# Expert up-weights kept on chip and copied per tile by an engine, instead of loaded per tile by DMA

## The chip, the cores and the metric

One core of a Trainium2 chip runs the kernel. The metric is the device time of one execution in microseconds (us). Five engines work side by side, each through its own list of instructions in order, and meet at semaphores: TensorE (PE, matrix products; PEld is its loading of weights), VectorE (DVE), ScalarE (ACT), GpSimd (POOL) and SyncE (SP, which here issues most DMAs). DMA engines move data between the chip's memory (DRAM) and the on-chip memory (SBUF). PE writes to PSUM, from which DVE and ACT read.

## The reference: what is computed

Eight sequences of 512 tokens with 128 features, all in float32, go through three layers, each with a residual: a routed feed-forward layer, a gated linear recurrence, and the same feed-forward layer again.

```
x = x + 0.5 * ffn(layernorm(x))
x = x + attn(layernorm(x))
x = x + 0.5 * ffn(layernorm(x))

def ffn(x):                                  # 8 experts, one per token
    xn  = rms_norm(x, scale)
    ids = argmin(dist2(xn, centroids))
    out = zeros_like(x)
    for e in range(8):
        a, g = split(xn @ up_w[e])           # up_w[e]: 128 x 512
        y = (a * silu(g)) @ down_w[e]        # down_w[e]: 256 x 128
        out = where(ids == e, y, out)
    return out + x
```

`attn` forms r, k, v by one product, takes exp(k), runs two decaying sums along the sequence, divides one by the other, multiplies by sigmoid(r) and projects.

## The kernel before

**Tokens are sorted by expert through DRAM.** `prepare` (L580) computes norms, scores and a row for each token of 260 values: its normalised features, half of its layer-norm output and residual, and its number. `route` (L647) finds each token's expert and its place in a table in DRAM; `scatter` (L714) writes 128 rows at a time there with an indirect DMA issued by POOL. `take` (L729) then divides the table into tiles of 128 rows that belong to one expert each and writes, for each tile, one integer to `place`: the tile's number plus 512 times its expert.

**Experts.** `experts` (L817) loads `place` into registers (L826), on SP for the loads and on PE for the down weights. `pair` (L847) handles two tiles at once:

- SP loads the tiles' rows to `xg` (L866, 130 KB a tile, 7 buffers of a pair) and their experts' up weights to `wup` (L873, 256 KB a tile, 3 buffers of a pair), both from addresses in registers;
- PE transposes the features (L879), ACT evicts them to `xgT` (L907);
- PE multiplies by the up weights (L884, eight products a tile, to the PSUM tile `h`);
- ACT applies silu (L916), DVE multiplies (L921), giving `sg`;
- PE multiplies by the down weights (L892, four products a tile), which all lie in SBUF (`wsb`) and are picked by PE's registers; the one PSUM area for it has room for one pair;
- DVE adds the half-residual (L928) and POOL scatters each tile's result to its tokens' places in DRAM (`send`, L934).

There are three tables: one for blocks (sequences) 0 to 3 and one for 4 to 7 in the first layer, with 23 tiles each, and one for all of the last layer with 39 tiles, of which 8, 8 and 4 are taken early, as soon as their rows are complete. That makes 85 tiles in 44 pairs. `finish` (L946) loads the blocks back, and `attention` (L953) runs the recurrence, mostly on DVE (L1008 to L1038), ACT and PE.

**The order of each engine's list** is decided at build time by `Plan` (L41 to L154). Each step is added with one or more ways, a way being an engine and an assumed cost, with the buffers it reads and writes, an optional due number per engine (`order`) and a lag. `schedule` places steps one after another where they could start first; a second way is taken only if the first way's engine would be free too late (L101). It tries 48 settings and keeps the shortest plan. Steps due FIRST (such as ACT's and DVE's steps of a pair, `soon`, L859) come ahead of others that could start as early. So the list of an engine after an edit can differ far from the edit.

Of the kernel before, what the change touches and what calls it, by code (L numbers as in the profile page):

```python
# [10 lines left out]
F32 = mybir.dt.float32  # L11
# [29 lines left out]
class Plan:  # L41
# [17 lines left out]
    def add(self, ways, reads=(), writes=(), order=None, part=False, lag=0.0, table=None):  # L59
        op = Op(ways, reads, writes, order or {}, lag, table)  # L60
        for b in reads:
            op.needs.update(b.writers)
            b.readers.append(op)
        for b in writes:
            op.needs.update(b.readers)
            if not (part and not b.readers):
                op.needs.update(b.writers)
            if b.readers or not part:
                b.readers, b.writers = [], []
            b.writers.append(op)  # L70
        op.needs.discard(op)
        self.ops.append(op)
# [85 lines left out]
def kernel(  # L158
# [36 lines left out]
    nc = tc.nc  # L195
    B, L, D = x_in.shape
    E, _, H2 = up_w.shape
    H = H2 // 2
    P = 128
# [22 lines left out]
    const = ctx.enter_context(tc.tile_pool(name="const", bufs=1))  # L222
# [8 lines left out]
    xb = [xpool.tile([P, NT, D], F32, tag=f"x{b}", name=f"x_{b}") for b in range(B)]  # L231

    wsb = const.tile([P, E * W], F32, tag="wsb", name="wsb")
    wrkv_sb = const.tile([P, 3 * P], F32, tag="wrkv_sb", name="wrkv_sb")
    wo_sb = const.tile([P, D], F32, tag="wo_sb", name="wo_sb")

# [17 lines left out]
        out=tri_f, in_=tri_f, pattern=[[-1, P]], compare_op=ALU.is_ge, fill=0.0,  # L254
# [50 lines left out]
    def buf(pool, shape, dtype, tag, n, count):  # L305

        slots[tag] = count
        return Buf(lambda: pool.tile(shape, dtype, tag=tag, name=f"{tag}_{n}", bufs=count), tag)
# [18 lines left out]
    add = plan.add  # L327
    FIRST, LATE = -10**6, 10**6
    EXP, SILU = "natural_log_exp_and_others", "silu_and_others"
    x_ = [Buf(lambda b=b: xb[b]) for b in range(B)]  # L330
    wd_, wr_, wo_, routing_, attending_ = (Buf(lambda w=w: w) for w in (wsb, wrkv_sb, wo_sb, None, None))
    for b in range(B):
        add([("SP", 1.15, lambda b=b: nc.sync.dma_start(
            out=xb[b], in_=x_in[b].rearrange("(t p) d -> p t d", p=P)))], [], [x_[b]], lag=2.5)
    for e in range(E):
        add([("SP", 0.6, lambda e=e: nc.sync.dma_start(
            out=wsb[:, e * W : (e + 1) * W].rearrange("p (c d) -> p c d", d=D),
            in_=down_w[e].rearrange("(c p) d -> p c d", p=P)))], [], [wd_], part=True, lag=2.5)
# [4 lines left out]
        out=bo_f[:, 0, :], in_=b_o.unsqueeze(0).to_broadcast([3, D])))], [], [bo_], lag=2.5)  # L343
# [69 lines left out]
    for j, v in enumerate((nu_log, gamma_log)):  # L413
        add([("ACT", 0.3, lambda j=j, v=v: nc.scalar.dma_start(
            out=arows[j : j + 1, :], in_=v.unsqueeze(0)))], [], [arows_], part=True, lag=2.2)
    add([("ACT", 0.3, lambda: nc.scalar.dma_start(
        out=arows[2:5, :], in_=b_rkv.rearrange("(j p) -> j p", p=P)))],
# [311 lines left out]
    def take(table, m: int):  # L729
# [62 lines left out]
        if last:  # L792
# [13 lines left out]
            add([("SP", 1.3 + 0.52 * E, zeros)], [fills], [fill_], lag=2.5)  # L806
            parts.append(fill_)
        experts(table, m, place, parts)

    def expert(place):  # L810
        return (place >> (PACK.bit_length() - 1)).with_bounds(min_val=0, max_val=E - 1)

    wdown = [wsb[:, c * D :] for c in range(NHC)]
    up_rows = up_w.rearrange("e p h -> p e h")
    npairs = [0]

    def experts(table, m: int, place, parts):  # L817

        downs, downs_ = [], Buf(None)
        spots = {}  # L820
        slots["regs"] = 2

        keep = []

        def load(engine, j0, j1):
            return nc.values_load_multi_w_load_instructions(  # L826
                place()[0:1, j0:j1], engines=(engine,), min_val=0, max_val=(E - 1) * PACK + table.tiles - 1,
                skip_runtime_bounds_check_because="no tile lies beyond the table",
            )[1]

        add([("PE", 0.1 * m, lambda: downs.extend(load(mybir.EngineType.PE, 0, m)))],
            [place], [downs_], {"PE": LATE + npairs[0] * 10 + 5})
        for j0 in range(0, m, LIST):
            j1 = min(j0 + LIST, m)
            at_ = Buf(None, "regs")

            def registers(j0=j0, j1=j1):
                spots.update(zip(range(j0, j1), load(mybir.EngineType.SP, j0, j1)))

            add([("SP", 1.3, registers)], [place], [at_], {"SP": LATE + npairs[0]})  # L840
            for j in range(j0, j1, 2):
                k = npairs[0]
                npairs[0] += 1
                pair(k, table, parts, keep, spots, at_, downs, downs_,
                     list(range(j, min(j + 2, j1))))

    def pair(k, table, parts, keep, spots, at_, downs, downs_, tiles):  # L847
        n = len(tiles)
        early = table.left > 0
        xg = buf(work, [P, 2, ROW], F32, "xg", k, 7)  # L850
        wup = buf(work, [P, 2, H2], F32, "wup", k, WUP)
# [7 lines left out]
        soon = {"ACT": FIRST + k, "DVE": FIRST + k}  # L859
# [12 lines left out]
        def weights(i, j):  # L872
            nc.sync.dma_start(  # L873
                out=wup()[:, i, :],
                in_=up_rows[:, ds(expert(spots[j]), 1), :])

        def features_first():
            for i in range(n):
                nc.tensor.transpose(ps_x()[:, ts(i, P)], xg()[:, i, :D], ident)  # L879
# [17 lines left out]
        for i, j in enumerate(tiles):  # L897
            add([("SP", 0.52, lambda i=i, j=j: rows(i, j))], [at_] + parts, [xg], {"SP": LATE + k},
                part=True, lag=2.3)
        for i, j in enumerate(tiles):  # L900
            add([("SP", 0.52, lambda i=i, j=j: weights(i, j))], [at_], [wup], {"SP": LATE + k},
                part=True, lag=3.8)
        add([("PE", 0.17 * n, features_first)], [xg], [ps_x],
            {"PE": LATE + 10 * k - 13}, lag=0.2)
        add(
# [156 lines left out]
    for i, (f, batches, taken) in enumerate(TABLES):  # L1062
        Table.order = i * LATE // 8
        table = Table(f"t{i}", f, [b for batch in batches for b in batch])
# [44 lines left out]
```

## Time and profile before

| | |
|---|---|
| timed runs, median of 3 | 306.41 us (305.02 to 306.7) |
| the profiled execution | 342.0 us, its recorded span 340.2 us |
| mean granted TensorE clock in it | 0.898 |
| busy in the span | PE 236.0, PEld 197.3, DVE 180.1, ACT 158.8, POOL 178.2 us |
| DMA traffic | 55.83 MB, 164 GB/s on the mean |
| of it, on SP's queue | 42.71 MB |
| up weights | 85 loads of 256 KB |

The profile is of one execution, and that one took longer than the timed runs, so times within it are compared with its own span. It gives, for each engine, what share of the span it was busy, also in 40 slices of 8.5 us as digits (tenths); groups of instructions with count, total and mean time, and the engine's idle time before them; the DMA issues; the waits and who ended them; and a timeline. In a group's name, `h<-xgT,wup` means: writes h, reads xgT and wup. A timeline line gives start, duration (both in us), engine, line, operation and operands, and in brackets how long the engine had been idle and what released it; SPq is SP's queue issuing DMAs. Consecutive alike instructions are merged (x16).

### The profile page before, as it was taken

The numbers are of one execution on the slowest core, as the hardware profiler recorded it, in microseconds if no ns is written. First come the engines' busy times: TensorE is split into PE (matmuls) and PEld (weight loads), VectorE is DVE, ScalarE is ACT, GpSimd is POOL, SyncE is SP. The second block draws the span as 40 slices with busy tenths as digits, with TensorE's granted clock in tenths as the row PEclk, the third lists the DMA queues.
The fourth block names the chain that finished last, engine by engine and source line by source line (L and its number), as shares of the span: only waits on it lengthen the run. The fifth ranks groups of instructions, "written<-read, shape, count | busy, mean of one in ns | idle before, by whom it ended". The sixth has DMA issues, their size and how long they took to land. (4 is left out here: it accounts for less than half of the span.)

```text
span 340.2 us, 5776 instructions
## 1 busy us (share of the span) xinstructions
PE 236.0 (69%) x1510; PEld 197.3 (58%) x1510; DVE 180.1 (53%) x604; ACT 158.8 (47%) x329; POOL 178.2 (52%) x258
## 2 busy tenths in 40 slices
PE   3566167197776995999773867799843495988870
PEld 2565157087666984877451633369742384987770
DVE  4786464121133227559898875989976431232230
ACT  4876652312122231897857385665866131222220
POOL 5377557235544544746271768403677544255563
PEclk9999999679999899999995876989975589899997
DMA  7824586496666799820003217250056578777710
GB/s 212 237 79 160 174 263 204 133 270 191 220 201 204 221 277 323 267 69 18 8 21 104 79 47 263 80 156 15 22 141 228 148 246 286 251 232 219 231 53 8
DMA packets 45139, 55.83 MB, mean 164 GB/s; under 512 B 6255, under 2 KB 31115, under 8 KB 45106
## 3 DMA queue, kind: packets, MB, share of 16 engines
q1 hardware_dynamic: 39286, 42.71, 42.7%
q0 software_dynamic: 5792, 12.73, 10.2%
q8 instruction: 13, 0.21, 0.3%
q14 instruction: 20, 0.16, 0.2%
q10 hardware_dynamic: 28, 0.01, 0.0%
HBM read 39.11 MB, written 17.68 MB: 167 GB/s over the span
## 5 line engine op out<-in xcount | busy, mean ns | idle before, releaser
L884 PE MATMUL h<-xgT,wup 128*128 128x128 f32 x680 | 90.4, 289 | 0.6 <-issue 0.5
L884 PEld LDWEIGHTS h<-xgT,wup 128*128 128x128 f32 x680 | 86.7, 206 | 1.7 <-issue 1.7
L716 POOL DMA_INDIRECT t<-xrow,posi_t x64 | 65.7, 1026 | 35.3 <-issue 17.3
L934 POOL DMA_INDIRECT yt<-ys,xg x46 | 50.8, 1105 | 56.3 <-DVE ys L928 28.1
L921 DVE TENSOR_TENSOR sg<-h,sg 128x512 f32<-128x512 f32 (+1 forms) x44 | 29.1, 670 | 84.7 <-ACT sg L916 65.9
L934 POOL DMA_INDIRECT out_dram<-ys,xg x39 | 39.4, 1009 | 51.5 <-DVE ys L928 36.9
L892 PE MATMUL ps_b<-wsb,sg 128*128 x340 | 49.6, 291 | 21.8 <-DVE ys L928 12.3
L916 ACT ACTIVATE sg<-h 128x512 f32<-128x512 f32 (+1 forms) x44 | 25.2, 582 | 75.5 <-PE h L884 22.9
L892 PEld LDWEIGHTS ps_b<-wsb,sg 128*128 128x128 f32 x340 | 43.8, 201 | 26.9 <-DVE ys L928 14.2
L907 ACT ACTIVATE xgT<-ps_a,cols 128x256 f32<-128x256 f32 (+1 forms) x44 | 20.4, 464 | 47.4 <-PE ps_a L879 24.7
L879 PE MATMUL ps_a<-ident,xg 128*128 128x128 f32 x85 | 20.9, 313 | 20.0 <-ACT xgT L907 10.4
L928 DVE SCALAR_TENSOR_TENSOR ys<-ps_b,xg 128x256 f32<-128x256 f32 (+1 forms) x44 | 18.0, 410 | 24.6 <-PE ps_a L879 10.5
L450 ACT ACTIVATE xrow<-x,nra,rs 128x128 f32<-128x128 f32 x64 | 26.3, 482 | 9.7 <-DVE nra L604 8.3
L622 PE MATMUL ps_b<-cw,xT 128*128 128x8 f32 x128 | 23.0, 312 | 8.3 <-ACT xT L467 4.4
L622 PEld LDWEIGHTS ps_b<-cw,xT 128*128 128x128 f32 x128 | 22.8, 270 | 9.8 <-ACT xT L467 4.9
L879 PEld LDWEIGHTS ps_a<-ident,xg 128*128 128x128 f32 x85 | 11.9, 156 | 25.9 <-ACT xgT L907 13.0
L450 ACT ACTIVATE xrow<-x,nra,one 128x128 f32<-128x128 f32 x64 | 26.1, 480 | 0.0
L689 PE MATMUL ps_b<-onehot_t,tri 128*128 128x32 f16 (+1 forms) x11 | 2.2, 197 | 24.6 <-DVE onehot_t L673 20.8
L152 ACT ACT_TABLE_LOAD x14 | 18.0, 1283 | 0.2
L525 PE MATMUL side_x<-ident,x 128*128 128x128 f32 x64 | 13.6, 354 | 4.9 <-ACT yr L505 2.4
L692 PEld LDWEIGHTS <-ones_h 128*128 128x128 f16 x11 | 1.2, 107 | 26.7 <-issue 26.6
L478 DVE BATCH_NORM_STATS2 bn_f<-x 128x6 f32<-128x128 f32 x64 | 13.6, 281 | 5.0 <-DMA x<-in_L_attn_inputs_dram 3.8
(156 smaller groups left out, 322.8 us busy)
## 6 DMA issues: line engine op xcount, KB each, us to landing
wup<-in_L_ffn_up_w_dram SPq DMA_DIRECT2D x85, 256.0 KB
xg<-t SPq DMA_DIRECT2D x85, 130.0 KB
t<-fill SPq DMA_DIRECT2D x27, 130.0 KB
x<-in_L_attn_inputs_dram SPq DMA_DIRECT2D x8, 256.0 KB
x<-yt SPq DMA_DIRECT2D x8, 256.0 KB
wsb<-in_L_ffn_down_w_dram SPq DMA_DIRECT2D x8, 128.0 KB
t<-xrow,posi_t POOLq DMA_INDIRECT x64
yt<-ys,xg POOLq DMA_INDIRECT x46
```

The source lines that it names most:

```text
L152: self.load_table(load)
L450: nc.scalar.activation(out()[:, t, :], src()[:, t, :], AF.Identity, bias=bias()[:, t : t + 1], scale=scale()[:, t : t + 1],)
L622: nc.tensor.matmul(ps_d()[:, ts(i * NT + t, E)], xT()[:, ts(t, P)], cw, start=True, stop=True)
L716: ordered(table, nc.gpsimd.indirect_dma_start(out=table.at()[:, :], out_offset=bass.IndirectOffsetOnAxis(ap=posi()[:, q : q + 1], axis=0), ...
L879: nc.tensor.transpose(ps_x()[:, ts(i, P)], xg()[:, i, :D], ident)
L884: nc.tensor.matmul(hp()[:, i, ts(c, P)], wup()[:, i, ts(c, P)], xgT()[:, ts(i, P)], start=True, stop=True,)
L892: nc.tensor.matmul(ps_y()[:, ts(i, D)], sg()[:, i, ts(c, P)], wdown[c][:, ds(expert(downs[j]) * W, D)], start=(c == 0), stop=(c == NHC - 1),)
L907: ("ACT", 0.2 + 0.13 * n, lambda: nc.scalar.activation(xgT()[:, : n * P], ps_x()[:, : n * P], AF.Copy, scale=scale_c)),
L916: [("ACT", 0.16 + 0.22 * n, lambda: nc.scalar.activation(sg()[:, :n, :], hp()[:, :n, H:], AF.Silu))],
L921: [("DVE", 0.1 + 0.28 * n, lambda: nc.vector.tensor_mul(sg()[:, :n, :], hp()[:, :n, :H], sg()[:, :n, :]))],
L928: add([("DVE", 0.1 + 0.18 * n, lambda: nc.vector.scalar_tensor_tensor(y()[:, :n, :], half(), 0.5, xg()[:, :n, D : 2 * D], ALU.mult, ALU.ad ...
L934: inst = nc.gpsimd.indirect_dma_start(out=table.result()[:, :], out_offset=bass.IndirectOffsetOnAxis(ap=xg()[:, i, 2 * D : 2 * D + 1].bitc ...
```

## The change

All eight experts' up weights get a place in SBUF, `usb`, 16 KB in each partition. Eight DMAs of 256 KB fill it at the start, added after the loads of x and before those of the down weights. For each tile, the SP load of `wup` from DRAM is replaced by a copy of 128x512 values from `usb` at an address in a register to the same rotating buffer `wup`. The step has two ways, DVE with an assumed cost of 0.4 us and ACT with 0.62, and it is due FIRST as the pair's other steps are. To address `usb`, `place` is also loaded to registers of ACT and DVE, once for each `take`. `wup` keeps its three buffers, and `up` (PE) reads them as before. `onchip` returns True for every table, so the old load is no longer used.

```diff
+    usb = const.tile([P, E * H2], F32, tag="usb", name="usb")
...
     for e in range(E):
+        add([("SP", 0.45, lambda e=e: nc.sync.dma_start(
+            out=usb[:, e * H2 : (e + 1) * H2], in_=up_w[e]))], [], [wu_], part=True, lag=2.5)
...
+    def onchip(table):
+        return True
...
     def experts(table, m: int, place, parts):
         downs, downs_ = [], Buf(None)
+        ups, ups_ = {"ACT": [], "DVE": []}, {"ACT": Buf(None), "DVE": Buf(None)}
...
+        if onchip(table):
+            for name, engine in ("ACT", mybir.EngineType.Activation), ("DVE", mybir.EngineType.DVE):
+                add([(name, 0.3 + 0.05 * m,
+                      lambda name=name, engine=engine: ups[name].extend(load(engine, 0, m)))],
+                    [place], [ups_[name]], {name: FIRST + npairs[0]})
...
+        def copies(i, j, name, copy):
+            copy(wup()[:, i, :], usb[:, ds(expert(ups[name][j]) * H2, H2)])
...
         for i, j in enumerate(tiles):
+            if onchip(table):
+                add(
+                    [
+                        ("DVE", 0.4, lambda i=i, j=j: copies(i, j, "DVE", nc.vector.tensor_copy)),
+                        ("ACT", 0.62, lambda i=i, j=j: copies(i, j, "ACT", nc.scalar.copy)),
+                    ],
+                    [wu_, ups_["DVE"], ups_["ACT"]], [wup], soon, part=True,
+                )
+                continue
             add([("SP", 0.52, lambda i=i, j=j: weights(i, j))], [at_], [wup], {"SP": LATE + k},
                 part=True, lag=3.8)
```

More of the change, by code (lines that the diff above doesn't have):

```diff
@@ L330 @@
     x_ = [Buf(lambda b=b: xb[b]) for b in range(B)]
-    wd_, wr_, wo_, routing_, attending_ = (Buf(lambda w=w: w) for w in (wsb, wrkv_sb, wo_sb, None, None))
+    wd_, wu_, wr_, wo_, routing_, attending_ = (
+        Buf(lambda w=w: w) for w in (wsb, usb, wrkv_sb, wo_sb, None, None))
     for b in range(B):
@@ L334 @@
             out=xb[b], in_=x_in[b].rearrange("(t p) d -> p t d", p=P)))], [], [x_[b]], lag=2.5)
+    for e in range(E):
+        add([("SP", 0.45, lambda e=e: nc.sync.dma_start(
+            out=usb[:, e * H2 : (e + 1) * H2], in_=up_w[e]))], [], [wu_], part=True, lag=2.5)
     for e in range(E):
@@ L843, in experts, with pair @@
                 npairs[0] += 1
-                pair(k, table, parts, keep, spots, at_, downs, downs_,
+                pair(k, table, parts, keep, spots, at_, downs, downs_, ups, ups_,
                      list(range(j, min(j + 2, j1))))
-    def pair(k, table, parts, keep, spots, at_, downs, downs_, tiles):
+    def pair(k, table, parts, keep, spots, at_, downs, downs_, ups, ups_, tiles):
         n = len(tiles)
```

## The prediction

> **What bounds the kernel now.** I read the 40 slices first, then the groups and issues, then the timeline of two expert stretches, then the waits and the chain. The slices (each 8.5 us; tenths busy) show three parts:
>
> ```profile
> PE   3566167197776995999773867799843495988870
> ...
> DVE  4786464121133227559898875989976431232230
> ...
> DMA  7824586496666799820003217250056578777710
> ```
>
> In the expert stretches (slices 8 to 15 and 33 to 39) TensorE (PE) and the DMA engines are high and VectorE (DVE) is at 1 to 3. The recurrence in between (slices 19 to 30) is DVE's: mostly 7 to 9, and DMA mostly 0 to 3. So the change takes from what is scarce in the outer parts and adds to what is scarce in the middle.
>
> ```profile
> L884 PE MATMUL h<-xgT,wup 128*128 128x128 f32 x680 | 90.4, 289 | 0.6 <-issue 0.5
> ...
> L716 POOL DMA_INDIRECT t<-xrow,posi_t x64 | 65.7, 1026 | 35.3 <-issue 17.3
> L934 POOL DMA_INDIRECT yt<-ys,xg x46 | 50.8, 1105 | 56.3 <-DVE ys L928 28.1
> ...
> wup<-in_L_ffn_up_w_dram SPq DMA_DIRECT2D x85, 256.0 KB
> ```
>
> 85 up-weight loads of 256 KB are 22.3 of 55.8 MB. An expert pair (two tiles) moves 2 x (256 + 130 + 64) KB = 0.92 MB. At the busiest slice, 323 GB/s, that is 2.85 us. GpSimd (POOL) sends two scatters a pair: 2 x (0.98 + 0.30 between them) = 2.56 us. PE's own pace is in the timeline of the last stage, where three pairs follow each other unhindered:
>
> ```profile
> 292.73 1.95 PE L884 MATMUL h<-xgT,wup 128*128 128x128 f32 x16
> ...
> 295.62 1.95 PE L884 MATMUL h<-xgT,wup 128*128 128x128 f32 x16
> ...
> 298.52 1.95 PE L884 MATMUL h<-xgT,wup 128*128 128x128 f32 x16
> ```
>
> 2.90 us a pair. DMA and PE are level; POOL is close behind. But most pairs of the profiled execution are slower, and the reason matters:
>
> ```profile
> 89.56 1.95 PE L884 MATMUL h<-xgT,wup 128*128 128x128 f32 x16
> ...
> 92.90 0.88 SPq L873 DMA_DIRECT2D wup<-in_L_ffn_up_w_dram  x2
> 92.91 0.60 ACT L916 ACTIVATE sg<-h 128x512 f32<-128x512 f32 x1 [5.51 <-PE h L884]
> ```
>
> This silu belongs to the pair before, whose matmuls ended at 88.6. It and the next weight load, which waits for the same matmuls, were both released at 92.9, while PE had gone on to the next pair. PE's signals came 4 us late, with PE's records in order. The waits show more of it: "ACT sg L916 <- remote: 18.9, 4, 7.4".
>
> How much of this is in the timed runs? The profiled execution took 342.0 us (span 340.2), the timed runs 306.4: 35.6 less. From the first expert matmul at 52.99 to 140 us there are 314 of L884's matmuls, 19.6 pairs; at 2.90 that is 57 of 87 us, so 30 are lost. From 270.4 to 328.9 there are 16 pairs, 46 of 58.5 us; 12 lost. The two losses sum to 42. If the late signals are the recording's doing and the 35.6 are these (I can't prove it), the timed runs lose only about 6.5 us to DMA and ramps in the expert stages. **That is the most that freeing the DMA engines can return: 306.4 - 6.5 = 300.** I take a third, -2 us, since the ramps (PE waits of 7.3 and 4.3 us for xg, whose rows are scattered first) remain.
>
> **What is removed.** 85 issues of 0.33 to 0.45 us on SP: SP waits for others most of the time; zero. 20.2 MB net of traffic: the -2 above. xg loads queue behind nothing of 256 KB any more: in the same -2.
>
> **The resident load.** 8 DMAs, 2 MB, behind x and ahead of the down weights: 2 MB at 212 to 237 GB/s (slices 1 and 2) shifts those and W_rkv, W_o, b_o by 9 us. The first down matmul is at 67.55, the bias split at 33, the first copy near 31; all land by about 25. Zero, and +1 if b_o were late.
>
> **Where the copies go.** In the order that the changed kernel is built to, all 85 copies are on DVE, none on ScalarE; ScalarE loads no registers either. That is the planner's choice: DVE's way comes first and is cheaper. One copy: the nearest row is L433, a copy from on-chip memory to on-chip memory of 128x1024 float32, 683 ns; a 128x5 copy (L423) took 156. The slope, 0.517 ns an element, gives 418 ns for 512. 85 x 0.418 = 35.5 us. Six register loads on DVE come with them. SP's loads of the same table (L826) took 0.22 to 0.71, PE's 0.50 to 3.48 (waits included); I take 0.6, 3.6 us in all. Register arithmetic in front of each copy: PE's runs ahead of its matmuls beside them; 0 to 0.08 each, taken as 0.
>
> **A rule against the change.** The Trainium skill's page "SBUF — State Buffer", section "Who interferes with whom", says that a float32 copy in on-chip memory can run in a mode that takes the port pair shared by VectorE and GpSimd; who comes first keeps it for a whole instruction and the other stands. The timeline has both directions:
>
> ```profile
> 45.17 0.68 DVE L433 COPY lam_l<-lam 128x1024 f32<-128x1024 f32 x1
> 45.48 1.26 POOL L716 DMA_INDIRECT t<-xrow,posi_t  x1 [5.09 <-DVE posi_t L704]
> ...
> 265.28 0.99 POOL L934 DMA_INDIRECT out_dram<-ys,xg  x1 [0.84 <-issue]
> ...
> 265.87 0.41 DVE L756 TENSOR_SCALAR ends_t<-ends_t 128x8 int32<-128x8 int32 x1
> ```
>
> The scatter that began under the copy took 1.26, not 0.96. The one-source DVE instruction that began 0.59 into a scatter took 0.41 instead of 0.17 and ended with it. But the same L756 at 52.35, 0.25 into a scatter, took 0.17. So the scatter holds the pair only in its later half. By the rule (0.98 of each 1.28 us held) a copy meets it 3 times in 4 and waits 0.49: 0.37 a copy, 0.75 a pair. By the rows (0.5 held) it is 0.4 x 0.25 = 0.10, 0.2 a pair. I take the rows. The upper end is the 3x128 bias casts (L349, L350), which beside scatters finished up to 1.2 us late. The lower end is zero.
>
> **Expert stages.** DVE a pair: product 0.69, result 0.42, two copies 0.84, locks 0.2: 2.15 of 2.90. Order on DVE: an older pair's result, the copies for pair k+3, the product of pair k. The copies wait for the up matmuls of pair k to leave the buffer; queued behind them is the product, which waits for those same matmuls and 0.6 of silu. So the product ends 0.45 later than before, 1.9 after the matmuls; the down matmuls that want it come 2.9 after (0.9 down, 0.2 transposes, 1.8 up of the next pair lie between). The result behind it frees the one down bank at 2.35: 0.55 in hand. Cover holds; if a copy waited 0.8, it is gone. POOL: 2.56 plus up to 0.3 of locks, 2.86, just under PE. For 36 uncovered pairs I put 0.05 each: +2.
>
> **Start.** The load and six copies (3.1 us) stand on DVE at 30.9 ahead of the factors of blocks 4 to 7. In exchange the bias split (33.4 to 41.9) moves behind the next routing. Zero, between -3 and +3.
>
> **The middle.** Eleven copies (4.6 us) of the second table's tail go between moments and products of the first recurrence; DVE is half idle to 145: +1. In the last table: a load and six copies (3.1) where DVE waited 2.4 us for `side_v` at 207: +0.7. Two copies in the recurrence, DVE at 100% there: +0.9. A load and six copies (3.1, with locks 3.7) near 250, ahead of the last block's recurrence. Its rows are wanted only after the six early pairs (17 us) from 270: +1. But POOL scatters blocks 4 and 5 then, and up to 0.3 for each copy goes to the rows that start the last expert stage: +1.4. Sum +5.
>
> **Sum**: -2 + 0 + 2 + 5 = +5. Against the profiled execution that is 342.0 + 5 = 347 if its late signals recur; the +5 contains none of them, so it carries over to the median: 306.4 + 5, rounded to 311.5.
>
> **Rivals.**
> 1. *Copies in DVE's scarce stretch, experts at PE's pace* (above): 308 to 318, 311.5. For: the slices. Against: DVE idle just where some land. Chance 0.45.
> 2. *DMA was the bound of the experts* (other side): from the point where a pair's 0.92 MB takes longer than PE's 2.90, that is below 317 GB/s; the mean of expert slices is nearer 230. The pace falls to PE's, and all 6.5 return, with the middle hidden at +0 to +2: 300 (295 to 304.8). Against: 2.90 at 292 to 301 with all loads running. Chance 0.23.
> 3. *The lock makes DVE or POOL the bound*: 0.8 a copy, DVE 2.15 - 0.2 + 1.6 = 3.55 a pair; 34 pairs x 0.65 = 22, plus 5: 333 (319 to 336). For: the bias casts. Chance 0.2.
> 4. *All hidden*: DMA's -4 against +4: 306. Chance 0.12. That the copies aren't made doesn't arise: the build has them.
>
> The range 8 in 10 leaves out the ends of 2 and 3: 299 to 327. A measurement here can tell about 0.5% (1.5 us) from no change. Faster: 0.23 of rival 2. Same: 0.12. Slower: 0.65.
>
> **What would show it.** Right: no wup DMA, DMA share near half in expert slices, PE pairs at 2.9; copies at 0.42 in quiet and to 0.9 beside scatters; DVE busy by 36 to 45 us more; the last expert stage begins later. Scatters longer than 0.98 show the lock on POOL. PE's idle before the down matmuls put down to DVE ys, at 0.5 or more a pair, shows rival 3. The late signals of PE may shrink in the new profile without the timed run gaining: I compare stages, not spans. I am wrong if the timed runs shared those late signals with the profiled one, since then DMA relief is worth far more than 6.5.

## The result, and the profile after

The changed kernel takes **310.11 us** (median of 4 runs, 309.1 to 311.73) beside 306.56 for the kernel before (4 runs, 305.02 to 307.09). The ratio is 1.014, with a 95% interval of 1.010 to 1.019: slower by 1.4%. The forecast was 311.5.

One thing must be known for the profiles. On some chips the kernel before takes about 340 us in every run, and on others about 306; the profile shown of before (342.0) is from the first sort, the profile after (310.12, span 308.4) from the second. Their spans are not compared here, only what each engine does, and ratios only between runs on one chip. A ratio leaves out executions more than 1.5% above their kernel's fastest; on the chip of 306.8 of the experiments this drops 25 of before's 49 (one took 302.26) and none of the change's 11, so there the means of all executions are given too.

The slices, groups and issues of the page after; each slice is 7.7 us:

```profile
PE   3765554799979999969732919699940867999980
...
DVE  3778498555645795992897786999987765565540
...
PEclk9999999999999999998955857999976759999995
DMA  7993638734355841003102002310011476445200
...
L721 POOL DMA_INDIRECT t<-xrow,posi_t x64 | 67.3, 1051 | 40.4 <-issue 27.4
...
L962 POOL DMA_INDIRECT yt<-ys,xg x46 | 49.4, 1075 | 23.5 <-DVE ys L956 11.8
...
L962 POOL DMA_INDIRECT out_dram<-ys,xg x39 | 40.2, 1030 | 35.2 <-DVE ys L956 23.7
L894 DVE COPY wup<-usb 128x512 f32 x85 | 33.9, 441 | 32.3 <-PE h L903 27.1
...
usb<-in_L_ffn_up_w_dram SPq DMA_DIRECT2D x8, 256.0 KB, 5.9
```

The copies are where the build had put them: 85 on DVE, 441 ns on the mean, and DVE's busy time is 213.8 us (180.1 before). The eight resident loads are the only up-weight DMAs; traffic fell from 55.83 to 35.61 MB. In the expert slices (9 to 15 and 34 to 38) DMA is now mostly at 3 to 5 tenths and PE mostly at 9. The recurrence (slices 20 to 32, DVE at 6 to 9) is still DVE's. The three kinds of scatter take 1051, 1075 and 1030 ns on the mean; before they took 1026, 1105 and 1009, and in the changed kernel's order without its copies (an experiment below) 1042, 1041 and 1000. So the copies lengthen a scatter by 0.01 to 0.03 us on the mean.

The timeline of the last expert stage, which held late signals before:

```profile
262.20 1.95 PE L903 MATMUL h<-xgT,wup 128*128 128x128 f32 x16
264.19 0.60 ACT L944 ACTIVATE sg<-h 128x512 f32<-128x512 f32 x1 [1.25 <-PE h L903]
264.19 0.87 DVE L894 COPY wup<-usb 128x512 f32 x2 [1.12 <-PE h L903]
...
264.98 0.68 DVE L949 TENSOR_TENSOR sg<-h,sg 128x512 f32<-128x512 f32 x1
...
265.10 1.95 PE L903 MATMUL h<-xgT,wup 128*128 128x128 f32 x16
267.08 0.60 ACT L944 ACTIVATE sg<-h 128x512 f32<-128x512 f32 x1 [1.25 <-PE h L903]
```

The matmuls end at 264.15, and silu and the copies both start at 264.19: 0.04 us late, not 4. A pair comes every 2.90 us, with DVE's two copies (0.87) beside it. The 27.1 us of idle time before the copies in the groups are DVE waiting for a buffer to come free, ahead of time; PE waits only 0.2 us for the copies in the whole profile.

DVE's register loads, line L836 (min/median/max in ns, first and last start):

```profile
L836 DVEq TENSOR_LOAD <-place_t x6: 344/1499/3882, 31.7 to 257.2; - x6
```

They are long: 3.88 us for the first table's 23 values at 31.7, ahead of the routing of blocks 4 to 7; 10.5 us for the six.

### The profile page after: what moved, and what is told of

Same layout as the page of the kernel before. It is cut to its first block, busy times and chain, and to the rows that moved or that the text cites. A ratio compares the mean times of both kernels' runs of the same rounds, so it can differ in the third digit from the quotient of the medians.

```text
span 308.4 us, 5682 instructions
## 1 busy us (share of the span) xinstructions
PE 226.9 (74%) x1510; PEld 190.6 (62%) x1510; DVE 213.8 (69%) x689; ACT 168.6 (55%) x335; POOL 177.0 (57%) x258
## 2 busy tenths in 40 slices
DMA packets 34048, 35.61 MB, mean 115 GB/s; under 512 B 5023, under 2 KB 29883, under 8 KB 34018
## 5 line engine op out<-in xcount | busy, mean ns | idle before, releaser
L721 POOL DMA_INDIRECT t<-xrow,posi_t x64 | 67.3, 1051 | 40.4 <-issue 27.4
L903 PE MATMUL h<-xgT,wup 128*128 128x128 f32 x680 | 86.2, 281 | 0.0
L903 PEld LDWEIGHTS h<-xgT,wup 128*128 128x128 f32 x680 | 82.9, 199 | 0.0
L962 POOL DMA_INDIRECT yt<-ys,xg x46 | 49.4, 1075 | 23.5 <-DVE ys L956 11.8
L962 POOL DMA_INDIRECT out_dram<-ys,xg x39 | 40.2, 1030 | 35.2 <-DVE ys L956 23.7
L894 DVE COPY wup<-usb 128x512 f32 x85 | 33.9, 441 | 32.3 <-PE h L903 27.1
L911 PE MATMUL ps_b<-wsb,sg 128*128 x340 | 47.1, 282 | 7.2 <-DVE sg L949 6.1
L911 PEld LDWEIGHTS ps_b<-wsb,sg 128*128 128x128 f32 x340 | 42.6, 195 | 10.9 <-DVE sg L949 7.1
L898 PE MATMUL ps_a<-ident,xg 128*128 128x128 f32 x85 | 19.3, 297 | 6.8 <-DMA xg<-t 5.9
L1078 PEld LDWEIGHTS side_o<-wo_sb,num 128*128 128x128 f32 x64 | 10.2, 229 | 17.0 <-DVE num L1043 12.7
L1078 PE MATMUL side_o<-wo_sb,num 128*128 128x128 f32 x64 | 10.3, 314 | 11.1 <-DVE num L1043 11.1
```

The source lines that it names most:

```text
L721: ordered(table, nc.gpsimd.indirect_dma_start(out=table.at()[:, :], out_offset=bass.IndirectOffsetOnAxis(ap=posi()[:, q : q + 1], axis=0), ...
L894: copy(wup()[:, i, :], usb[:, ds(expert(ups[name][j]) * H2, H2)])
L903: nc.tensor.matmul(hp()[:, i, ts(c, P)], wup()[:, i, ts(c, P)], xgT()[:, ts(i, P)], start=True, stop=True,)
L911: nc.tensor.matmul(ps_y()[:, ts(i, D)], sg()[:, i, ts(c, P)], wdown[c][:, ds(expert(downs[j]) * W, D)], start=(c == 0), stop=(c == NHC - 1),)
L962: inst = nc.gpsimd.indirect_dma_start(out=table.result()[:, :], out_offset=bass.IndirectOffsetOnAxis(ap=xg()[:, i, 2 * D : 2 * D + 1].bitc ...
L1078: nc.tensor.matmul(ps_o()[:, ts(t, P)], num()[:, ts(i * NT + t, P)], wo_sb, start=False, stop=(t == NT - 1),)
```

## The experiments

Theories when these began. **Main:** the price is DVE's own work on its path (copies and register loads), and the DMA relief is worth about nothing. **Rival, large against large:** the relief is several us, and the price larger still. **Rival, order:** the list of every engine is planned anew for the changed steps, and that order is what costs. The lock as a rival had fallen: the scatters above are hardly longer.

Four chips were met in the experiments; the table gives what before takes on each. "Stretch" is from the product `sg` of the first table's last pair (the 12th) to that of the 31st pair, in the last stage: the second table, the recurrence and the last routing lie between. "First" is the 1st pair's product.

| kernel | before there | ratio, 95% interval | first | stretch |
|---|---|---|---|---|
| before | 342.0 | - | 66.8 | 170.4 |
| half load | 342.4 | 0.998 (0.996 to 1.001) | 66.5 | 168.9 |
| no up loads, old order | 339.6 | 0.976 (0.974 to 0.979) | 65.6 | 166.2 |
| no loads, no copies, own order | 342.4 | 0.987 (0.982 to 0.992) | 66.4 | 172.0 |
| first layer only | 342.4 | 1.021 (1.015 to 1.028) | 71.2 | 180.6 |
| last layer only | 342.4 | 1.010 (1.005 to 1.016) | 67.1 | 178.1 |
| copies on ACT | 339.6 | 1.008 (1.005 to 1.010) | 74.7 | 175.8 |
| the change again | 306.8 | 1.011 (1.008 to 1.015) | 55.6 | 174.5 |
| its order, quarter copies | 306.8 | 1.006 (1.003 to 1.009) | 54.8 | 174.0 |
| its order, no register loads | 306.8 | 1.012 (1.008 to 1.016) | 54.9 | 174.5 |
| its order alone | 306.8 | 1.005 (1.002 to 1.009) | 53.8 | 175.8 |

One more run is the kernel before against itself on the chip of 342.0: 0.9999 (0.9966 to 1.0031). It shows what no change measures, and its stretch was 169.6.

### Half of each up load

Only 256 of the 512 columns are loaded, and the up projection uses them twice. The orders stay as they were.

```diff
-                out=wup()[:, i, :],
-                in_=up_rows[:, ds(expert(spots[j]), 1), :])
+                out=wup()[:, i, : H2 // 2],
+                in_=up_rows[:, ds(expert(spots[j]), 1), : H2 // 2])
...
-                        hp()[:, i, ts(c, P)], wup()[:, i, ts(c, P)], xgT()[:, ts(i, P)],
+                        hp()[:, i, ts(c, P)], wup()[:, i, ts(c % 2, P)], xgT()[:, ts(i, P)],
```

> The kernel before, with only the first 256 of each expert's 512 up columns loaded (128 KB a tile, not 256) and used twice: 11 MB less traffic, every engine's list as before, nothing added. Main theory (the experts of the timed runs are already at PE's pace of 2.9 us a pair, so DMA relief is worth little): 304 to 306.5. Rival (DMA is the bound of the experts in the timed runs, and the change's net +3.6 is a large relief less a large cost): 298 or less. Its profile should have fewer of PE's late signals, so its profiled execution should come near its timed runs in both cases.

0.998: traffic is 44.69 MB in place of 55.83, and nothing came of it. On a chip of 340, bytes are not what holds the experts.

### No loads and no copies

All tiles use expert 0's resident up weights in place. Nothing is copied, DVE loads no registers, and the planner makes an order of its own.

```diff
-                        hp()[:, i, ts(c, P)], wup()[:, i, ts(c, P)], xgT()[:, ts(i, P)],
+                        hp()[:, i, ts(c, P)], usb[:, ts(c, P)], xgT()[:, ts(i, P)],
```

> The changed kernel without any copy and without its register loads: all tiles use expert 0's resident up weights in place, so nothing but the down half depends on the expert. The plan is made anew. Main theory: at best 6.5 us under before, 300 to 306. Rival (large relief, large cost): 297 or less. If it is not below before at all, the cost of the change isn't the copies' time but the order that the planner makes without the loads.

0.987: 1.3% is what the change could have won there, in this order, if its copies had cost nothing. As a ratio, that is what the main theory had forecast (300 to 306 us beside 306). That PE reads each tile's own expert in `usb`, at an address in a register, wasn't tried.

### The change in one layer only

```diff
     def onchip(table):
-        return True
+        return table.f == 0
```

(46 of 85 tiles copied; `table.f == 1` is the other run, 39 tiles.)

> Copies for the 46 tiles of the first layer, loads from DRAM for the 39 of the last. Main theory (the costly copies are those of the last table, in the scarce stretch of DVE and ahead of the last expert stage, +3 to +4; those of the first layer cost about 1 to 2): 306 to 308. Rival (the first layer's copies cost as much, by the lock or by the order): 309 to 312.

> Loads from DRAM for the 46 tiles of the first layer, copies for the 39 of the last. Main theory: 309 to 311, most of the change's +3.6. Rival: 305 to 307.

1.021 and 1.010. The first is the opposite of what the main theory wanted. It also doesn't separate the layers: each run has an order of its own. In the first, the pairs of the first table go faster than before (12 pairs in 36.6 us, 43.1 before), and then the stretch is 10 us longer, the last table's first early pair coming at 251.4 in place of 228.8. This is what the order rival says.

### The change with parts of DVE's work taken out, in its own order

Four runs on one chip. The order of the other engines is the changed kernel's in all. The last three leave parts out: quarter copies take 128 columns, which the up projection uses four times; without register loads, the copies take expert 0's weights for all tiles; the order alone has neither copies nor register loads, and PE reads expert 0's weights in place. This changes values, not work: the number of tiles is fixed when the kernel is built.

```diff
# quarter copies
-            copy(wup()[:, i, :], usb[:, ds(expert(ups[name][j]) * H2, H2)])
+            copy(wup()[:, i, :P], usb[:, ds(expert(ups[name][j]) * H2, P)])
-                        hp()[:, i, ts(c, P)], wup()[:, i, ts(c, P)], xgT()[:, ts(i, P)],
+                        hp()[:, i, ts(c, P)], wup()[:, i, :P], xgT()[:, ts(i, P)],
# no register loads
-                      lambda name=name, engine=engine: ups[name].extend(load(engine, 0, m)))],
+                      lambda: None)],
-            copy(wup()[:, i, :], usb[:, ds(expert(ups[name][j]) * H2, H2)])
+            copy(wup()[:, i, :], usb[:, :H2])
# order alone: no register loads, and
-            copy(wup()[:, i, :], usb[:, ds(expert(ups[name][j]) * H2, H2)])
+            pass
-                        hp()[:, i, ts(c, P)], wup()[:, i, ts(c, P)], xgT()[:, ts(i, P)],
+                        hp()[:, i, ts(c, P)], usb[:, ts(c, P)], xgT()[:, ts(i, P)],
```

> The changed kernel once more, unaltered, so that the variants have it beside them. Its ratio to before was 1.014 where before takes 306. Two theories of the experiments so far differ on it where before takes 342: if the price is DVE's own work on the path (copies and register loads), it is the same number of microseconds on any chip, 3 to 5, so 1.010 to 1.016. If the chip's late PE signals add to the price, the sum of the two halves tried alone (2.1% and 1.0%) is seen, 1.025 to 1.035.

> The changed kernel with copies of 128 instead of 512 columns in the same order and with the same register loads (the up projection uses those 128 columns four times). A copy should take about 0.20 us instead of 0.42, so DVE has 18 us less work. If the length of the copies is the price: 3 to 4 us below the changed kernel, near the kernel before. If the price is the register loads (10.5 us of DVE, 3.9 of them ahead of the routing) or the order made anew: within 1.5 us of the changed kernel.

> The changed kernel with the copies at a fixed address (all tiles use expert 0's up weights), so that DVE loads no registers; all else in the same order. If the price is the register loads: 3 to 5 us below the changed kernel, most of it at the start, where DVE's load of 23 registers took 3.88 us at 31.7 and the routing's second half came 7.4 us later than in the profile of before. If the copies or the order are the price: within 1.5 us of the changed kernel.

> The order of the changed kernel with neither copies nor register loads on DVE (the up projection reads expert 0's resident weights in place for all tiles), and no up loads per tile. What is left against before is the order made anew, the eight resident loads at the start and the DMA relief. If DVE's added work is the whole price: 1 to 2% below before (0.98 to 0.99), as in the run without loads and copies that made its own plan (0.987). If the order is the price: 1.00 to 1.015, at most 1.5 us below the changed kernel.

The medians are 310.35, 308.66, 311.23 and 307.12 us, beside 306.8; the means are 310.36, 309.15, 311.38 and 307.34, beside 306.73. Three things follow.

First, register loads cost nothing that can be measured: 1.012 without them, 1.011 with them, and the mean without them is 1.0 us longer (95% interval -0.1 to +2.2), though they are 10.5 us of DVE.

Second, all of DVE's added work costs 3.0 us (95% interval 2.1 to 3.9): that is the mean of the change less the mean of its order alone, compared directly. Their two ratios to before differ by less, 0.6% or 1.9 us, but each also carries before's scatter. The copies' length is a large part of it: quarter copies (260 ns each) get back 1.2 us by the means, 1.7 by the medians and 2.3 by the executions that the ratio keeps. That is less than the 3 to 4 expected if length were all of the price. Where does the price lie? The `sg` lines of the timelines, first of the change, then of its order alone (1st, 12th, 31st and 44th pair):

```profile
55.62 0.68 DVE L949 TENSOR_TENSOR sg<-h,sg 128x512 f32<-128x512 f32 x1
...
87.42 0.41 DVE L949 TENSOR_TENSOR sg<-h,sg 128x256 f32<-128x256 f32 x1
...
261.94 0.68 DVE L949 TENSOR_TENSOR sg<-h,sg 128x512 f32<-128x512 f32 x1
...
298.00 0.42 DVE L949 TENSOR_TENSOR sg<-h,sg 128x256 f32<-128x256 f32 x1 [0.55 <-ACT sg L944]
```

```profile
53.84 0.69 DVE L949 TENSOR_TENSOR sg<-h,sg 128x512 f32<-128x512 f32 x1 [0.91 <-ACT sg L944]
...
85.83 0.42 DVE L949 TENSOR_TENSOR sg<-h,sg 128x256 f32<-128x256 f32 x1 [0.55 <-ACT sg L944]
...
261.65 0.69 DVE L949 TENSOR_TENSOR sg<-h,sg 128x512 f32<-128x512 f32 x1 [2.21 <-ACT sg L944]
...
297.89 0.42 DVE L949 TENSOR_TENSOR sg<-h,sg 128x256 f32<-128x256 f32 x1 [0.55 <-ACT sg L944]
```

The experts start 1.8 us later with the copies and loads ahead of the routing (55.6; in the first profile of the change it was 56.4). From there the twelve pairs take the same time (31.8 and 32.0). In the stretch the profiled execution of the order alone loses what it had won. But this one's time, 309.84, was the longest of its 14, 2.5 us above their mean, while the change's profiled execution (309.95) was near its mean. So 1.8 us of the price show at the start, and where the other 1.2 lie these two profiles can't show.

The stretch does say that DVE's work sets little of it. The windows from 88 to 262, the change and its order alone (PE, PEld, DVE, ACT, POOL busy, each with its count, then clock, DMA share and GB/s):

```profile
88.00:262.00 174.00, 127.21 (x768) 96.48 (x767) 133.78 (x386) 107.67 (x196) 87.28 (x112) 0.85 0.29 87
```

```profile
88.00:262.00 174.00, 127.26 (x761) 96.64 (x760) 120.77 (x347) 107.40 (x196) 85.09 (x110) 0.84 0.28 85
```

That is 13 us less of DVE work, and no shorter a stretch in this execution. Even if all of its 2.5 us above the mean lay here, its usual stretch would be 173.3, which is 1.2 us less than with the copies.

Third, with DVE's work gone, the changed kernel's order, its resident loads at the start and its DMA relief together come to 1.005 (1.002 to 1.009), or 1.002 (0.999 to 1.005) by the means: no gain, and between nothing and 1.6 us of loss. Neither theory came out whole. The ratio is in the 1.00 to 1.015 that the order theory had expected and not in the 0.98 to 0.99 of the main one; but the run is 3.0 us below the changed kernel, where the order theory had allowed 1.5. So DVE's work is a price, on top of an order that with all its relief gains nothing. All four runs were on a chip of 306, so what the whole change costs on one of 340 stays open.

### Before once more, and without its up loads

The first is the kernel before, for its profile. The second leaves out all 85 up loads; PE multiplies by resident down weights of the same shape, and every other instruction keeps its place.

```diff
         def weights(i, j):
-            nc.sync.dma_start(
-                out=wup()[:, i, :],
-                in_=up_rows[:, ds(expert(spots[j]), 1), :])
+            pass
...
-                        hp()[:, i, ts(c, P)], wup()[:, i, ts(c, P)], xgT()[:, ts(i, P)],
+                        hp()[:, i, ts(c, P)], wsb[:, ts(c, P)], xgT()[:, ts(i, P)],
```

> The kernel before, unaltered, for a profile beside runs of about 307. The prediction took the late PE signals of its profile (sg up to 4 us after its matmuls) for the recording's doing. If that is so, this profile shows them again and a span near 340. If they belong to the state of the chip in which before takes 342, this profile has a span near 305, expert pairs at 2.9 us, and a last expert stage that begins within 2 us of 254.

> The kernel before in its own order, with every up load of a tile taken out (the up projection multiplies by resident down weights in their place, the same shapes); DVE, ACT, POOL and PE run the same instructions in the same order, and 85 DMAs of 256 KB and SP's 85 issues are gone. If the DMA relief is worth nothing, as the half load said (0.998): 0.995 to 1.002 of before. If the full load hides a relief that the half load did not show, as the 0.987 of the run without loads and copies could be read: 0.983 to 0.99.

The profile again shows 342.2 us and the late signals, on a chip where all 19 timed runs of before took 340 to 346:

```profile
89.54 1.95 PE L884 MATMUL h<-xgT,wup 128*128 128x128 f32 x16
92.85 0.89 SPq L873 DMA_DIRECT2D wup<-in_L_ffn_up_w_dram  x2
92.86 0.60 ACT L916 ACTIVATE sg<-h 128x512 f32<-128x512 f32 x1 [5.49 <-PE h L884]
```

So the late signals are not the recording's doing. They go with the chips on which before takes 340. For each pair, take how long its silu starts after its matmuls have ended in the records and ACT is free. Over the 44 pairs of this profile that sums to 33.2 us, 12 of them by more than 1 us. In the five profiles from chips of 306 it is 1.4 us each, never more than 0.04 for one pair. The difference between the chips, 35 us, is of this size, as the prediction had supposed; that the one makes the other isn't shown.

On such a chip the loads' removal gives 0.976, 8.4 us. That is against the expectation drawn from the half load. The main theory's "relief is worth nothing" holds for bytes and not for the loads as such. The late time of the silus goes with it: 33.2 us in before, 32.5 with half the bytes, 20.0 without the loads (20.7 in the run without loads and copies). What in the loads makes the signals later isn't shown. SP's waits may have a part. First before, then the half load (SPq is SP's queue; total, times, longest):

```profile
SPq L873 <- PE ps_a L879: 12.9, 8, 3.0
...
SPq L873 <- PE side_v L993: 4.0, 1, 4.0
SPq L873 <- PE h L884: 3.5, 2, 1.8
...
SPq L873 <- remote: 2.3, 3, 1.8
```

```profile
SPq L873 <- PE h L884: 13.5, 6, 3.9
...
SPq L873 <- PE ps_a L879: 6.0, 5, 2.3
...
SPq L873 <- remote: 2.1, 2, 1.8
```

An up load waits in SP's queue until PE's late signal frees one of the three buffers, and the next tiles' row loads stand behind it: 22.7 us in before, 21.6 with half the bytes, and none without the loads. That fits both results. But PE's own waits for row loads before its transposes fall only from 7.5 to 5.5 us, and the number of packets behaves like the waits (39286 on that queue in both, 27046 without the loads). So the queue as the cause is argued and not shown.

The run without loads and copies, in an order of its own, gave 0.987; the same removal in the old order is worth 1.1% more. The late time is alike in both (20.7 and 20.0), so the difference is the new order's, or in part that of the resident loads at the start (the first pair comes 0.8 us later). The stretches say the same, all on chips of 340: 166 to 170 us in five executions of the old order (the first profile's 169.8 and the 169.6 of before against itself among them), 172 to 181 in the four new orders.

### The copies on ACT

```diff
-            for name, engine in ("ACT", mybir.EngineType.Activation), ("DVE", mybir.EngineType.DVE):
+            for name, engine in (("ACT", mybir.EngineType.Activation),):
...
-                        ("DVE", 0.4, lambda i=i, j=j: copies(i, j, "DVE", nc.vector.tensor_copy)),
```

> The changed kernel with all 85 copies on ACT in place of DVE, in an order made for it. A copy should take 0.6 to 0.7 us on ACT, some 55 us in all; ACT was busy 55%, and in the full expert stages some 1.1 of 2.9 us a pair. If DVE's copies are the changed kernel's price and ACT has the room: 0 to 3 us off the changed kernel, 1.00 to 1.01 of before. If an engine ahead of the routing and in the middle stage is what is short, whichever it is: at or above the changed kernel, 1.01 to 1.03, with ACT's xrow and softmax steps later.

1.008 (1.005 to 1.010). A copy takes 0.62 us on ACT. With the copies ahead of ACT's row steps the first pair comes at 74.7 in place of 66.8. ACT has room in the expert stages (the first twelve pairs take 36.2 us, 43.1 before), and the stretch is again longer, 175.8. The number is the one forecast if ACT has the room, but the changed kernel itself ran on no chip of 340. On that chip nothing is won by moving them, and no version here that computes the whole layer beat the kernel before.

## Why the prediction was right, and where it wasn't

The sign and the size came out, 311.5 against 310.1, but the size in part by luck: the price of DVE's work was put too high and the relief too high as well, and the two errors largely cancel.

- **"If the late signals are the recording's doing"**: wrong. They go with the chip: before takes about 340 in all its runs there, and the recorded execution of the changed kernel (310.12) took no longer than its others. The consequence drawn, that the timed runs near 306 don't have them, agrees with the profile after (0.04 us late on such a chip), though no profile of before is from a chip of that sort. The size supposed for them, 35.6 us, is near the 33 measured.
- **DMA relief, "I take a third, -2 us"**: failed as a net term. On the chip of the timed sort, relief, resident loads and order together were +0.3 us by the medians, +0.6 by the means and +1.6 by the ratio (1.005). On a chip of 340 the loads' removal gave -8.4 us, more than the 6.5 that the prediction called the most for the timed runs. Its own warning, that relief is worth more where signals are late, is what was seen. There the bytes were not the reason: half of them gone gave nothing.
- **The order itself**: missing. The prediction read the new order only for where the copies stand in it. Of what relief, loads and order make together, how much is the order (on the chips of 340 a price of about 1%) and how much a relief set against it stays open: before's order without up loads ran on no chip of 306.
- **Copies, 85 x 0.418 = 35.5 us**: 33.9 us of busy time (441 ns on the mean, overlaps merged), median 424. Right; DVE's busy time rose by 33.7, just under the 36 to 45 forecast with locks. So was "the rows" for the lock, though 80 of the 85 copies ran beside a scatter: 401 ns at the least and 441 on the mean is 0.04 a copy, where the Trainium skill's "SBUF — State Buffer", section "Who interferes with whom", read as holding for a whole instruction, had given 0.37. The prediction took 0.10.
- **Register loads, 3.6 us**: 10.5 us, mis-sized threefold because PE's own loads (up to 3.48) were taken for waits. The register arithmetic before a copy, taken as 0, was 0.09 us on DVE's queue. Neither did harm: without both nothing was won.
- **Start, zero between -3 and +3**: 1.8 us, inside the range, and the one part of DVE's price that has a place.
- **Expert stages, +2**: zero; the twelve pairs take 31.8 us with copies and 32.0 without. The cover held, as the prediction had argued, at 2.90 us a pair. It held with more in hand: silu and copies start together, so the product ends 1.5 us after the matmuls and not 1.9.
- **The middle, +5**: mis-sized. DVE's slices at 9 looked scarce, yet 13 us less of DVE work in that stretch didn't shorten it in the profiled execution, and all of the price that isn't at the start is 1.2 us.

In sum: 7 us of DVE price and -2 of relief were forecast. Measured were about 3.0 us of DVE price and +0.3 to +1.6 where the relief should have been. Of the rivals, "the lock" was refuted on the timed sort of chip. Of "DMA was the bound" the faster kernel was refuted there; a relief hidden by a price of the order was not. A fifth case, the order made anew, was not among them.

## What to carry to other kernels

Where a planner writes each engine's list, an edit comes with a new order: run the new order with the edit's work taken out, before giving the edit the credit or the blame. A load that halves in bytes without effect may still cost time in another way, so test a transfer by removing it as well as by shrinking it. Compare variants of one order with each other, and not only each with the kernel before. Make sure that the profile read and the times explained are from chips on which the same kernel takes the same time.

## What was not expected of the hardware

- One kernel takes 306 us on some chips and 340 to 342 on others, at a mean granted clock of 0.92 and 0.89. On the slow ones PE's signals reach ACT and SP up to 4 us after the matmuls in the records have ended, on the others 0.04 us. Why was not found.
- A register load of 23 values took DVE 3.88 and 2.39 us, of 19 values 2.68, of eight 0.59 and 0.61, of four 0.34.
- A copy of 128x512 float32 takes 0.42 us on DVE and 0.62 on ACT; with 128 columns on DVE, 0.23 (medians).
